# A four-layer network on one core: the deformable layer from windows to dense sampling matrices, the shift layer from one dense product to two block-diagonal ones

## The chip, the core and the metric

The kernel runs on one core of a Trainium2 chip (trn2). A core has a matrix engine (TensorE, "PE" in the profile, with its weight loads listed apart as "PEld"), a vector engine (VectorE, "DVE"), an activation engine (ScalarE, "ACT"), a general engine (GpSimd, "POOL") and a queue engine (SyncE, "SP") that only issues transfers here. Each engine works through its own list of instructions in order and waits on semaphores for the others. Transfers are carried out by 16 DMA engines; SP and ACT both issue them.

The metric is device time in microseconds, the median of three runs. The span in the profile goes from the first to the last instruction.

## The reference

An image batch x of shape (8, 384, 32, 32), fp32, goes through four layers, each of the form x = x + layer(group_norm(x)):

- Layer 0 is a selective state-space layer (Mamba) over the 1024 positions of an image, with 768 inner channels and 16 states.
- Layer 1 is a deformable layer. The 384 channels are split into three groups of 128, with kernel sizes K = 3, 5 and 7.
- Layer 2 is a state-space layer again, with layer norm before and an MLP behind.
- Layer 3 is a learned shift: the channels form 48 positions of 8 channels each; every position has its own displacement.

Layers 1 and 3 are the ones touched. Cut to the core:

```python
# layer 1, one group: K*K taps, each with its own offset field
offsets = conv2d(x, ow, ob, pad)                      # 2*K*K maps
for k in range(K * K):                                # ky, kx: the tap's place
    py, px = gy + ky + offsets[2*k], gx + kx + offsets[2*k+1]
    acc += bilinear_sample(x, py, px) * w[k]          # zero outside the image
out = conv2d(acc, pw, pb, 0)                          # pointwise
# all three groups: out * sigmoid(fc2(relu(fc1(mean))) + fc2(relu(fc1(max))))

# layer 3: integer displacement, then a depthwise 5x5 Gaussian, normalised
disp[c, y, x] = x[c, y - dy, x - dx]                  # zero outside
kernel = exp(-(|(j, i) + sub|**2) / (2 * 0.5**2)); kernel /= kernel.sum()
out = depthwise_conv(disp, kernel)
```

Bilinear sampling at (py, px) is a sum over all pixels (y, x) of the image with the weights max(0, 1 - |py - y|) times max(0, 1 - |px - x|). So a tap can be written as a product of the image, as a 128 channels x 1024 pixels matrix, with a 1024 x 1024 sampling matrix, in 8 tiles of 128 pixels. The Gaussian of layer 3 is a product of a factor in y and a factor in x.

## The kernel before

`tile_net` calls the layers one after the other; the images x1, x2 and x3 between them lie in DRAM. Instructions are written in program order against tiles from pools, and a framework places them on the engines' lists and inserts the waits. A tile of a pool with `bufs=n` comes free for its n-th successor when its last reader is done. The order of the lists is therefore fixed when the kernel is built.

**Layers 0 and 2** (`ssm_layer`, lines 139 to 292) loop over the 8 images; within an image over two groups of three blocks of 128 channels, and within those over the 16 states. Each step has an exponential on ACT (L231), a product on POOL (L233), a scan and a product on DVE (L234, L235) and an accumulation on TensorE (L237).

**Layer 1** is there twice. `deform_fast` is the one that runs. For every image and group it has preparation steps (`prep_steps`: group norm, the offset convolution L606, the positions L621, their store to DRAM L626, transposed copies of the image L657) and main steps (`main_steps`). It assumes that offsets are small (RAD: 2, 3 and 4 pixels). Up to four taps share the 128 partitions, 32 pixels each: a cell of 4 rows by 8 columns. Such a cell only reaches the output pixels in a window around it, so the sampling matrix is built and multiplied for the window alone: L717 and L722 make the row factor, L703 and L709 the column factor, L753 their product for the window (90 to 900 elements per partition), L736 the image times the tap's weight, and L767 the product into the accumulator. The preparation of the next block is placed between the main steps of the present one by costs and due times written in the code (PACE, FIRST, the costs of the steps). The largest offset of each block goes to `far`; after the loop it becomes a flag, which `tile_net` reads back. Only where it is set does `deform_layer` run, in a branch.

`deform_layer` and `deform_block` (lines 341 to 475) make no assumption on the offsets. A block convolves its group out of a padded copy, adds the grid, stores the positions `pos` to DRAM (`posd`), and transposes the image into 8 tiles `xt` of 128 pixels. Then, for each tap, it loads the two rows of positions broadcast to 128 partitions (`pyx`, 1 MB) and the tap's weights (`wk`), multiplies the image by the weights on POOL (`xk`), and builds the whole sampling matrix in three steps of 2, 3 and 3 tiles (STEPS): the first step takes its Relu on ACT, the others use two DVE instructions. Two products of 512 columns follow for every tile. The tiles `sm` have four buffers, `pyx`, `xk`, `wk` and `hx` two. In the profiled execution none of this ran.

**Layer 3** (`shift_layer`, lines 830 to 938) normalises and transposes all images into `xt` (lines 881 to 896). Per position the partitions hold 64 rows (8 channels x 8 images); the shift and Gaussian are one 1024 x 1024 matrix, built in 8 tiles from the factors in y and x (L929) and multiplied (L932, 16 products per position). The result is added to x (L936) and stored by 8 transfers of 32 KB (L938).

Of the kernel before, what the change touches and what calls it, by code (L numbers as in the profile page):

```python
# [8 lines left out]
F32 = mybir.dt.float32  # L9
AF = mybir.ActivationFunctionType  # L10
# [5 lines left out]
P = 128  # L16
# [15 lines left out]
CPP = 8  # L32
NT = L // P
# [3 lines left out]

RAD = {3: 2, 5: 3, 7: 4}  # L40
CONV = {3: (4, 32, L // 4), 5: (2, 64, HL), 7: (1, P, L)}
NCONV = {3: 1, 5: 4, 7: 14}
PACE = 1.6
FIRST = 9.8
NX = 4
NB = 5
HXN, HYN, SMN = 2080, 1792, 896

def box(y, x, h=2, w=2):
    return [(y + i, x + j) for i in range(h) for j in range(w)]


QUADS = {
    3: [box(-1, -1), [(-1, 1), (0, 1), (1, 0), (1, 1)], [(1, -1)]],
    5: [box(y, x) for y in (-2, 0) for x in (-2, 0)] + [box(2, -2, 1, 4), box(-2, 2, 4, 1), [(2, 2)]],
    7: [box(-3, -3), box(-3, -1), box(-1, -3, 1, 4), box(-3, 2), box(-1, 2), box(-3, 1, 4, 1)]
    + [box(0, -3), box(2, -3), box(0, -1, 4, 1), box(2, 0), box(2, 2), box(1, 0, 1, 4), [(0, 0)]],
}  # L60
# [9 lines left out]

def taps_of(K):
    return [(y + K // 2) * K + x + K // 2 for q in QUADS[K] for y, x in q]

# [5 lines left out]
class Net:  # L79
    def __init__(self, ctx: ExitStack, tc: tile.TileContext, ins, out, nb):  # L80
# [4 lines left out]
        self.mm = ctx.enter_context(tc.tile_pool(name="mm", bufs=2, space=PSUM))  # L85
        self.dram = ctx.enter_context(tc.tile_pool(name="dram", bufs=2, space=DRAM))
# [15 lines left out]
    def group_norm(self, x, xn):  # L102
# [26 lines left out]
        rstd = small.tile([P, G], F32, name="gn_rstd")  # L129
        nb = small.tile([P, G], F32, name="gn_nb")  # L130
# [3 lines left out]
        nc.vector.scalar_tensor_tensor(nb, grp[:, :, 0], -1.0, rstd, ALU.mult, ALU.mult)  # L134
        for g in range(G):
            nc.vector.tensor_scalar(
                xn[:, g, :], x[:, g, :], rstd[:, g : g + 1], nb[:, g : g + 1], ALU.mult, ALU.add
            )


    def ssm_layer(self, li, src, dst):
        tc, nc, ins = self.tc, self.nc, self.ins
        mlp = li == 2
        with ExitStack() as ctx:
# [3 lines left out]
            self.acc = ctx.enter_context(tc.tile_pool(name=f"acc{li}", bufs=3, space=PSUM))  # L148
# [191 lines left out]
    def deform_layer(self, src, dst):  # L340
        tc, nc, ins = self.tc, self.nc, self.ins
        with ExitStack() as ctx:
# [3 lines left out]
            self.acc = ctx.enter_context(tc.tile_pool(name="acc1", bufs=3, space=PSUM))  # L346
# [130 lines left out]
    def deform_fast(self, src, dst):  # L477
        tc, nc, ins = self.tc, self.nc, self.ins
        with ExitStack() as ctx:
            wp = ctx.enter_context(tc.tile_pool(name="w1f", bufs=1))  # L480
            self.q1 = ctx.enter_context(tc.tile_pool(name="q1", bufs=1))
            self.q2 = ctx.enter_context(tc.tile_pool(name="q2", bufs=2))
            self.win_acc = ctx.enter_context(tc.tile_pool(name="win_acc", bufs=1, space=PSUM))
            self.f = {}
            for g, K in enumerate(KS):
                K2, (n, st, cols) = K * K, CONV[K]
                rows = 2 * K2
                ow = wp.tile([P, K2, rows if n == 1 else st], F32, name=f"fow{K}")
                ob = wp.tile([P, 1], F32, name=f"fob{K}")
                obk = wp.tile([P, 1], F32, name=f"fobk{K}")  # L490
                grid = wp.tile([P, cols], F32, name=f"fgrid{K}")
                for t in (ob, obk, grid) + ((ow,) if n > 1 else ()):
                    nc.gpsimd.memset(t, 0.0)
                nc.sync.dma_start(out=ow[:, :, :rows], in_=ins[f"ow{K}"])
                for i in range(n):
                    r = slice(i * st, i * st + rows)
                    nc.sync.dma_start(out=ob[r], in_=ins[f"ob{K}"])
                    nc.sync.dma_start(out=obk[r], in_=ins["c_cols"][:rows, Q_K + g : Q_K + g + 1])
                    nc.sync.dma_start(out=grid[r], in_=ins["c_grid"][:rows, i * cols : (i + 1) * cols])
                nc.vector.tensor_tensor(obk, obk, ob, ALU.add)  # L500
                nq = K2 // 4
                wk = wp.tile([P, nq + 1, P], F32, name=f"fwk{K}")
                for t in range(4):
                    nc.sync.dma_start(
                        out=wk[H * t : H * (t + 1), :nq, :],
                        in_=ins[f"dw{K}"][t : 4 * nq : 4, :].partition_broadcast(H),
                    )
                nc.sync.dma_start(out=wk[:, nq, :], in_=ins[f"dw{K}"][4 * nq, :].partition_broadcast(P))

                nc.vector.tensor_scalar(wk, wk, -1.0, None, ALU.mult)  # L510
                self.f[K] = (ow, ob, obk, grid, wk)
            pwt = wp.tile([P, G, P], F32, name="pwt")
            nc.sync.dma_start(out=pwt, in_=ins["pw"].rearrange("g c o -> c g o"))
            pwb = wp.tile([P, G], F32, name="pwb")
            nc.sync.dma_start(out=pwb, in_=ins["pwb"])
            f1 = wp.tile([P, G, RK], F32, name="f1")
            nc.sync.dma_start(out=f1, in_=ins["fc1"].rearrange("(k p) o -> p k o", p=P))
            f2 = wp.tile([RK, C], F32, name="f2")
            nc.sync.dma_start(out=f2, in_=ins["fc2"])
            self.cell = wp.tile([P, 12], F32, name="cell")  # L520
            nc.sync.dma_start(out=self.cell, in_=ins["c_cell"])
            self.zero = wp.tile([P, HL], mybir.dt.bfloat16, name="zero")
            nc.gpsimd.memset(self.zero, 0.0)
            self.far = wp.tile([P, 4 * self.nb], F32, name="far")
            nc.gpsimd.memset(self.far, -1.0)


            mains, preps, at, now = [], [], [], 0.0
            state = {}
            for b in range(self.nb):  # L530
                for g in range(G):
                    s = {} if g else {"b": b}
                    state[g] = s
                    s["prev"] = state[0]
                    m = self.main_steps(b, g, s, (pwt, pwb, f1, f2), src, dst)
                    mains.append((now, m))
                    preps.append(self.prep_steps(b, g, s, src))
                    now += sum(c for c, _ in m)
            end = now
            for i in reversed(range(len(preps))):  # L540
                end = min(end, mains[i][0])
                first = mains[i - 1][0] + FIRST if i else 0.0
                for j, (cost, fn) in enumerate(reversed(preps[i])):
                    end -= PACE * cost

                    at.append((max(end, first) if j < 3 else end, i, fn))
            at.reverse()
            for i, (now, m) in enumerate(mains):
                for cost, fn in m:
                    while at and (at[0][0] <= now or at[0][1] <= i):  # L550
                        at.pop(0)[2]()
                    fn()
                    now += cost
            bad = self.small.tile([P, 1], F32, name="bad")
            nc.vector.reduce_max(bad, self.far, axis=AX.X)
            nc.vector.tensor_scalar(bad, bad, 0.0, None, ALU.is_gt)
            ones = self.small.tile([P, 1], F32, name="ones")
            nc.gpsimd.memset(ones, 1.0)
            ps = self.psum("ps_bad", rows=1, n=1)
            nc.tensor.matmul(ps, ones, bad, start=True, stop=True)  # L560
            flag = self.const.tile([1, 1], mybir.dt.int32, name="flag")
            nc.vector.tensor_copy(flag, ps)
            return flag

    @staticmethod
    def sub(ap, off, dims):
        return bass.AP(tensor=ap.tensor, offset=ap.offset + off, ap=[list(ap.ap[0])] + [list(d) for d in dims])


    def prep_steps(self, b, g, s, src):  # L570
        nc, K = self.nc, KS[g]
        K2, pad = K * K, K // 2
        n, st, cols = CONV[K]
        ow, ob, obk, grid, _ = self.f[K]

        def load():
            xn = self.q1.tile([P, G, L], F32, name="fxn")
            nc.sync.dma_start(out=xn, in_=src(b))
            self.group_norm(xn, xn)
            s["xn"] = xn  # L580

        def xg():
            return s["prev"]["xn"][:, g, :]


        taps = [(0, 0)] + [
            (y, x) for y in range(-pad, pad + 1) for x in range(-pad, pad + 1) if (y, x) != (0, 0)
        ]
        nh = 2 if n == 1 else 1
        m = HL if n == 1 else cols  # L590
        rows = m // W
        width = 2 * K2 if n == 1 else st
        used = width * n
# [439 lines left out]
```

## Time and profile before

| | |
|---|---|
| median of 3 runs | 16312.42 us (16312.03 to 16312.46) |
| profiled execution | 16312.03 us, span 16310.3 us |
| granted TensorE clock, mean | 0.803 of full |
| busy share of the span | PE 66%, DVE 74%, ACT 29%, POOL 30% |
| instructions | 92702 |

In a group row, "out<-in" names the tiles written and read, then come the shape of the output and input, the count, total busy time in us and the mean in ns of one instruction, and after the last bar the idle time of that engine just before them and what ended it. "fp32" products appear as two records each: L237 has 1536 x 2 products and 6144 records. A matmul's duration overlaps that of the next one, so the rate is read from the busy sum, which counts overlap once. Idle time of an engine that isn't the bottleneck costs nothing.

### The profile page before, as it was taken

How to read it: one execution, taken by the hardware profiler on the slowest of the kernel's cores; microseconds unless marked ns; L12 is line 12 of the kernel's file. 1: busy time of each engine (PE TensorE's matmuls, PEld its weight loads, DVE VectorE, ACT ScalarE, POOL GpSimd, SP SyncE). 2: the span in 40 equal slices, each digit the busy share in tenths (PEclk: the TensorE clock that was granted, in tenths of full speed). 3: DMA queues.
4: the chain of work that ended last, by engine and by line, in shares of the span. 5: the costliest groups of instructions: out<-in, count | busy, mean ns of one | idle time of the engine just before them, and what ended most of it. 6: DMA issues, size and time to landing. Idle time of an engine off the chain costs nothing. (4 is left out here: it accounts for less than half of the span.)

```text
span 16310.3 us, 92702 instructions
## 1 busy us (share of the span) xinstructions
PE 10784.7 (66%) x33010; PEld 5823.2 (36%) x33010; DVE 12014.2 (74%) x10304; ACT 4758.4 (29%) x6104; POOL 4889.3 (30%) x1652
## 2 busy tenths in 40 slices
PE   5545465454565698888885474747474747474699
PEld 2212122121221366666663141414141414141442
DVE  7787877878778678778887848484848484848577
ACT  2222222222222255555553222222222222222210
POOL 4454533535434200000002515151515152524200
PEclk7777777777776799999997787878787878786889
DMA  1111111111111222233332101010101010101111
GB/s 65 52 59 52 54 55 49 57 52 58 54 43 57 71 76 75 73 79 78 78 77 76 57 32 57 30 59 29 57 32 57 29 57 32 57 26 57 42 46 35
DMA packets 231328, 888.16 MB, mean 54 GB/s; under 512 B 33266, under 2 KB 41106, under 8 KB 207176
## 3 DMA queue, kind: packets, MB, share of 16 engines
q1 hardware_dynamic: 221000, 844.41, 16.6%
q10 hardware_dynamic: 9856, 37.75, 0.6%
q8 instruction: 261, 4.28, 0.1%
q14 instruction: 211, 1.73, 0.0%
HBM read 824.19 MB, written 57.87 MB: 54 GB/s over the span
## 5 line engine op out<-in xcount | busy, mean ns | idle before, releaser
L237 PE MATMUL y<-hs,ident 128*128 128x512 f32 x6144 | 4016.6, 818 | 4683.9 <-DVE hs L235 4683.9
L234 DVE TENSOR_TENSOR_SCAN hs<-da,hs 128x1024 f32<-128x1024 f32 x1536 | 5456.3, 3575 | 1112.2 <-POOL hs L233 1112.2
L233 POOL TENSOR_TENSOR hs<-du,bc 128x1024 f32<-128x1024 f32 x1536 | 4874.5, 3198 | 4615.4 <-PE y L237 3281.3
L237 PEld LDWEIGHTS y<-hs,ident 128*128 128x128 f32 x6144 | 1572.2, 267 | 7121.3 <-DVE hs L235 4890.8
L231 ACT ACTIVATE da<-dt,na 128x1024 f32<-128x1024 f32 x1536 | 1763.8, 1148 | 6492.8 <-DVE hs L234 6403.3
L235 DVE TENSOR_TENSOR hs<-hs,bc 128x1024 f32<-128x1024 f32 x1536 | 1951.7, 1295 | 16.5
L767 PE MATMUL wacc<-fsm,fxk 128*128 128x221 f32 (+34 forms) x10624 | 1680.6, 316 | 226.5 <-DVE fsm L753 220.8
L193 POOL MEMSET xp<- 128x2 f32 x96 | 10.0, 106 | 5701.7 <-ACTq L956 3169.4
L767 PEld LDWEIGHTS wacc<-fsm,fxk 128*128 128x128 f32 x10624 | 1580.4, 196 | 353.5 <-DVE fsm L753 260.9
L753 DVE TENSOR_TENSOR fsm<-fhy,fhx 128x170 f32<-128x170 f32 (+42 forms) x3216 | 1169.4, 426 | 261.0 <-PE wacc L767 255.7
L289 DVE SCALAR_TENSOR_TENSOR x<-ps_m,vec,x 128x256 f32<-128x256 f32 x96 | 46.4, 483 | 1191.4 <-PE ps_m L285 1191.4
L717 ACT ACTIVATE fhy<-fpyx,cell 128x416 f32<-128x416 f32 (+9 forms) x1280 | 655.3, 576 | 728.2 <-DVE fsm L753 728.2
L606 PE MATMUL ps_off<-fxn,fow 128*32 128x248 f32 (+19 forms) x2944 | 832.0, 522 | 2.1 <-issue 1.9
L736 DVE TENSOR_TENSOR fxk<-fxt,fwk 128x1024 f32<-128x1024 f32 x640 | 759.5, 1216 | 37.3 <-PE wacc L767 24.4
L932 PE MATMUL sacc<-sm,xt 128*64 128x512 f32 x1536 | 669.2, 597 | 32.6 <-DVE xr L936 31.7
L247 PE MATMUL ps_z<-xn,win 128*128 128x512 f32 x1152 | 582.1, 660 | 118.9 <-DVE dt L304 118.9
L197 PE MATMUL ps_in<-xn,win 128*128 128x512 f32 x1152 | 535.0, 625 | 50.9 <-DVE xn L331 34.6
L929 DVE TENSOR_TENSOR sm<-kr 128x1024 f32<-128x1024 f32 x384 | 463.6, 1221 | 135.6 <-PE sacc L932 135.5
L277 PE MATMUL ps_h<-xn,w 128*128 128x256 f32 x2304 | 504.6, 379 | 4.9 <-ACT hid L281 4.9
L285 PE MATMUL ps_m<-hid,w 128*128 128x256 f32 x2304 | 502.5, 379 | 0.0
L262 PE MATMUL ps_o<-u,wout 128*128 128x512 f32 x1152 | 497.0, 592 | 0.0
L606 PEld LDWEIGHTS ps_off<-fxn,fow 128*98 128x98 f32 (+2 forms) x2944 | 354.4, 147 | 377.6 <-issue 355.6
(163 smaller groups left out, 8299.5 us busy)
## 6 DMA issues: line engine op xcount, KB each, us to landing
bc<-bcd SPq DMA_DIRECT2D x512, 1024.0 KB
fpyx<-fposd SPq DMA_DIRECT2D x640, 256.0 KB
x<-x ACTq DMA_DIRECT2D x16, 1536.0 KB
fpyx<-fposd SPq DMA_DIRECT2D x24, 1024.0 KB
x<-x SPq DMA_DIRECT2D x16, 1536.0 KB
x<-in_x SPq DMA_DIRECT2D x8, 1536.0 KB
fxn<-x SPq DMA_DIRECT2D x8, 1536.0 KB
fxr<-x SPq DMA_DIRECT2D x24, 512.0 KB
```

Of the source, the lines that this page charges most:

```text
L231: nc.scalar.activation(da, dt[:, j, :], AF.Exp, scale=na[:, d0 + j, n : n + 1])
L233: nc.gpsimd.tensor_tensor(hs, du[:, j, :], bc[:, 0, :], ALU.mult)
L234: nc.vector.tensor_tensor_scan(hs, da, hs, 0.0, ALU.mult, ALU.add)
L235: nc.vector.tensor_tensor(hs, hs, bc[:, 1, :], ALU.mult)
L237: nc.tensor.matmul(ys[j][:, s], self.ident, hs[:, s], start=(n == 0), stop=(n == NS - 1))
L247: nc.tensor.matmul(ps, win[:, k, DI + d * P : DI + (d + 1) * P], xn[:, k, s], start=(k == 0), stop=(k == G - 1),)
L606: nc.tensor.matmul(o[:, ya - r0 : yb - r0, xa:xb], ow[:, (dy + pad) * K + dx + pad, :], x3[:, ya + dy : yb + dy, xa + dx : xb + dx], start ...
L717: nc.scalar.activation(hy[:, at : at + (yb - ya) * W], pyx[:, 0, ya * W : yb * W], AF.Abs, bias=bias)
L736: nc.vector.tensor_tensor(t, s[q], wk[:, j : j + 1, :].to_broadcast([P, 2 * NX, P]), ALU.mult)
L753: nc.vector.tensor_tensor(self.sub(sm, at, [(r * w, n), (w, r), (1, w)]), self.sub(hy, hy_at[by] + xa, [(r * W, n), (W, r), (1, w)]), self ...
L767: nc.tensor.matmul(a[:, ya - 4 * o : yb - 4 * o, xa:xb], k, self.sub(sm, sm_at[by], [(w, yb - ya), (1, w)]), start=False, stop=False,)
L932: nc.tensor.matmul(acc[:R, s], xt[:, t, p * R : (p + 1) * R], smf[:, s], start=(t == 0), stop=(t == NT - 1),)
```

## The change

The diff has two parts. In layer 1, `deform_fast`, `prep_steps`, `main_steps`, `excite`, their tables and the branch are taken out, and `deform_layer` is called for every run; its own code stays as it was, except that the PSUM pool `acc` is now made once for the network instead of once per layer (3 buffers as before). The taps of the weights are in their natural order again. In layer 3, the partitions hold four channels of one image at a time, 32 rows each (`(i y)`), and the free dimension 8 images x 2 channel quartets x 32 columns. The factor in y is a 128 x 128 block-diagonal matrix with four equal blocks of 32 x 32, and so is the factor in x. The first product contracts the rows and leaves the result transposed, with columns on the partitions; the second contracts the columns and turns it back. Group norm's scale and shift are gathered in a table `tab` and applied to the tile as it is loaded. `group_norm` is split, so that the statistics (`gn_stats`) can be taken alone. Layer 2 stores its result by image instead of by channel.

```diff
-    far = net.deform_fast(by_sample(x[1]), by_sample(x[2]))
-    with tc.If(net.nc.values_load(far[0:1, 0:1]) > 0):
-        net.deform_layer(by_sample(x[1]), by_sample(x[2]))
-    net.ssm_layer(2, by_sample(x[2]), by_channel(x3))
-    net.shift_layer(by_channel(x3), x3.rearrange("c b l -> (c b) l"), out)
+    net.deform_layer(by_sample(x[1]), by_sample(x[2]))
+    net.ssm_layer(2, by_sample(x[2]), by_sample(x[3]))
+    net.shift_layer(by_sample(x[3]), x[3], out)
...
-            xt = wp.tile([P, NT, C * nb], F32, name="xt")
...
-                self.group_norm(x, x)
+                self.gn_stats(x, rn[:, 0, b, :], rn[:, 1, b, :])
...
+            for t in range(2):
                 for g in range(G):
+                    nc.vector.tensor_tensor(
+                        sel, hi, rn[:, t, :, g].unsqueeze(2).to_broadcast([P, nb, nq]), ALU.mult
+                    )
+                    nc.tensor.matmul(
+                        ps, cst[:, T_LO : T_LO + P], sel.rearrange("p b q -> p (b q)"), start=True, stop=True
+                    )
+                    nc.scalar.copy(tab[:, t, g].rearrange("p b q -> p (b q)"), ps)
...
+                bd = p2.tile([P, M2, IG, W], F32, name="bd", tag="bd")
+                for i in range(IG):
+                    nc.scalar.activation(bd[:, :, i, :], kr, AF.Copy, scale=grp[:, i : i + 1])
                 for n in range(PC):
                     p = p0 + n
-                    nc.sync.dma_start(out=xr, in_=src[p * R : (p + 1) * R, :])
-                    for t in range(NT):
-                        nc.vector.tensor_tensor(sm, my, mx, ALU.mult)
-                        for h, s in halves():
-                            nc.tensor.matmul(
-                                acc[:R, s], xt[:, t, p * R : (p + 1) * R], smf[:, s],
-                                start=(t == 0), stop=(t == NT - 1),
-                            )
-                    nc.vector.tensor_tensor(xr, xr, acc[:R, :], ALU.add)
-                    for c in range(CPP):
-                        nc.sync.dma_start(out=dst[:, p * CPP + c, :], in_=xr[c * nb : (c + 1) * nb, :])
+                    xr = p2.tile([P, nb, NJ, W], F32, name="xr", tag="xr", bufs=3)
+                    for j in range(NJ):
+                        c = p * CPP + j * IG
+                        nc.sync.dma_start(
+                            out=xr[:, :, j, :],
+                            in_=src[:, c : c + IG, :].rearrange("b i (y x) -> (i y) b x", x=W),
+                        )
+                    for op, t in ((ALU.mult, 0), (ALU.add, 1)):
+                        nc.vector.tensor_tensor(
+                            xa, xr if t == 0 else xa,
+                            tab[:, t, g, :, q : q + NJ].unsqueeze(3).to_broadcast([P, nb, NJ, W]), op,
+                        )
+                    for k in range(0, HL, P):
+                        nc.tensor.matmul(ps[:, k : k + P], xaf[:, k : k + P], my, start=True, stop=True)
+                    nc.scalar.copy(yt, ps)
+                    for k in range(0, HL, P):
+                        nc.tensor.matmul(ps2[:, k : k + P], yt[:, k : k + P], mx, start=True, stop=True)
+                    nc.vector.tensor_tensor(xrf, xrf, ps2, ALU.add)
+                    for j in range(NJ):
+                        c = p * CPP + j * IG
+                        nc.scalar.dma_start(
+                            out=dst[:, c : c + IG, :].rearrange("b i (y x) -> (i y) b x", x=W),
+                            in_=xr[:, :, j, :],
+                        )
```

`deform_block`, which every image and group now goes through, has this loop over the taps (as it stood before, unchanged):

```python
for k in range(K2):
    pyx = p2.tile([P, 2, L], F32, name="pyx", tag="pyx")
    nc.sync.dma_start(out=pyx, in_=posd[2 * k : 2 * k + 2, :].partition_broadcast(P))
    ...
    nc.gpsimd.tensor_tensor(xk, xt, wk.unsqueeze(1).to_broadcast([P, NT, P]), ALU.mult)
    nc.scalar.activation(hx, pyx[:, 1, :], AF.Abs, bias=self.col(Q_XN))
    nc.scalar.activation(hx, hx, AF.Relu, bias=self.col(Q_ONE), scale=-1.0)
    for t0, t1, on_act in STEPS:                       # tiles 0-1, 2-4, 5-7
        for i in range(n):
            nc.scalar.activation(sm[:, i, :], pyx[:, 0, :], AF.Abs, bias=self.col(Q_YN + t0 + i))
        if on_act:
            nc.scalar.activation(sm, sm, AF.Relu, bias=self.col(Q_ONE), scale=-1.0)
            nc.vector.tensor_tensor(sm, sm, hxb, ALU.mult)
        else:
            nc.vector.tensor_scalar(sm, sm, 1.0, 0.0, ALU.subtract, ALU.min)
            nc.vector.scalar_tensor_tensor(sm, sm, -1.0, hxb, ALU.mult, ALU.mult)
        for i in range(n):
            for h, s in halves():
                nc.tensor.matmul(acc[:, s], xk[:, t0 + i, :], sm[:, i, s], ...)
```

## The prediction

> **What bounds the kernel now.** I read the 40 slices first, then cut the span at the four layers with the table of windows, then took unit costs from the groups by line. The four rows are layer 0 (state space), layer 1 (deformable), layer 2 (state space with MLP) and layer 3 (shift). Columns are start:end, length, busy time of PE, PEld, DVE, ACT and POOL with their instruction counts, granted TensorE clock, DMA share and GB/s.
>
> ```profile
> 0.00:5533.00 5533.00, 3077.45 (x5472) 1238.35 (x5472) 4367.55 (x2305) 1358.13 (x1338) 2438.41 (x826) 0.74 0.15 54
> 5533.00:8713.00 3180.00, 2764.24 (x15250) 2138.10 (x15250) 2482.55 (x4788) 1685.57 (x2825) 3.89 (x13) 0.94 0.30 78
> 8713.00:15437.00 6724.00, 4171.74 (x10271) 2147.31 (x10272) 4515.28 (x2511) 1616.83 (x1839) 2446.96 (x814) 0.78 0.13 45
> 15437.00:16310.30 873.30, 771.25 (x2018) 299.46 (x2016) 648.83 (x701) 97.83 (x102) 0.00 (x0) 0.91 0.17 46
> ```
>
> Layer 1 takes 3180 us with PE and DVE both near full, and POOL free; layer 3 takes 873 us and is TensorE's. The change touches only these two. The order of instructions of the changed kernel is the old one line for line in both state-space layers, so their 5533 + 6724 us stay.
>
> The unit costs, from the groups by line with shapes kept apart (count | busy us, mean ns | idle before):
>
> ```profile
> L262 PE MATMUL ps_o<-u,wout 128*128 128x512 f32 x1152 | 497.0, 592 | 0.0
> L929 DVE TENSOR_TENSOR sm<-kr 128x1024 f32<-128x1024 f32 x384 | 463.6, 1221 | 135.6 <-PE sacc L932 135.5
> L722 DVE TENSOR_SCALAR fhy<-fhy 128x1344 f32<-128x1344 f32 x80 | 68.1, 851 | 3.7 <-ACT fhy L717 3.7
> L722 DVE TENSOR_SCALAR fhy<-fhy 128x1600 f32<-128x1600 f32 x64 | 63.0, 984 | 16.6 <-ACT fhy L717 16.6
> L307 DVE SCALAR_TENSOR_TENSOR sp_e<-sp_w,sp_e 128x1024 f32<-128x1024 f32 x96 | 116.6, 1214 | 0.0
> L703 ACT ACTIVATE fhx<-fpyx,cols 128x1024 f32<-128x1024 f32 x24 | 27.6, 1148 | 4.6 <-DMA fpyx<-fposd 2.9 <-issue 1.7
> ```
>
> An fp32 product is two records: 576 products in L262, 497.0 us, so 0.86 us each back to back, loads hidden. Tensor-tensor runs at 1.04 ns an element; tensor-scalar at (984-851)/256 = 0.52, fixed part 0.15 us. And who holds up whom, from the tile view of hs (min/median/max ns):
>
> ```profile
> L233 POOL TENSOR_TENSOR hs<-du,bc x1536: 2330/2886/4439, 83.0 to 15255.5; 128x1024 f32<-128x1024 f32 x192
> L234 DVE TENSOR_TENSOR_SCAN hs<-da,hs x1536: 2257/4366/4483, 90.1 to 15264.1; 128x1024 f32<-128x1024 f32 x192
> ```
>
> The scan takes 2.26 us alone and 4.37 beside a POOL product: it stands still for 2.11 us, nearly the whole POOL instruction.
>
> **What the Trainium skill says.** "SBUF — State Buffer", section Who interferes with whom: GpSimd's one SBUF port pair is VectorE's second; a VectorE instruction with two SBUF inputs, or in a two-port mode, and a GpSimd one that reads SBUF exclude each other for a whole instruction. The 2.26/4.37 us above agree. "VectorE: DVE Perf Modes", section The perf-mode tier table: fp32 tensor-scalar has a 2x mode, tensor-tensor none; 0.52 against 1.04 ns agree. "TensorE: Matmul & The Clock Gate", section Part 1: The HAM clock gate: an idle TensorE drops to half clock and needs some 3.4 us of work to come back; the 0.74 of layer 0 and 0.94 of layer 1 fit. "DMA: Bandwidth & Descriptors", section Specifications: line rate needs runs of 512 B or more, below it a read-modify-write is done. Loads here do well with less (200-byte runs of the weights fow: 2125 packets in 2.2 us, nearly all engines busy, about 15 ns each on 16 engines); short stores do not occur.
>
> **Part A, layer 1: windows out, dense sampling in.** Removed: 3180 us with everything in it, also the planned interleaving of the next block's convolution with the present block's taps, and the flag that `tile_net` reads back at its end. Added: `deform_block` 24 times, with 83 taps per image, so 664 taps. One tap costs, engine by engine:
>
> PE: 16 products of 128x512 at 0.86 = 13.7 us.
>
> DVE: one tensor-tensor of 2048 elements, then twice a tensor-scalar and a scalar-tensor-tensor of 3072. Back to back, an instruction starts N x 1.04 ns + 0.07 us after the one before (two L736 of 1024 take 2.34 us). So 2.20 + 2 x (1.75 + 3.27) = 12.24 us; the 1.75 is the full 0.52 x 3072 + 0.15, since the next instruction reads its result.
>
> POOL: the product xk, 1024 elements like L233: 2.33 us alone. All five DVE instructions have two SBUF inputs or the 2x mode, so by the lock it adds 2.1 us to DVE: 14.35 us.
>
> ACT: ten activations of 1024, one of 2048. Four L717 of 416 take 1.97 us with 0.63 for one, so a start every 0.45 = 416 x 0.833 ns + 0.10. Thus 0.95 per 1024, 1.81 for 2048, one wait of 0.2: 11.5 us. Its 1 MB of positions per tap is 73 GB/s, less than layer 1 moves now.
>
> DVE and POOL together set the beat, PE close behind at 13.7; I take 14.5 with waits. 664 x 14.5 = 9628 us.
>
> Between blocks nothing overlaps: on PE the order is convolution, transposes, all taps, pointwise product, next convolution. The convolutions are 166 products per image: 166 x 0.86 x 8 = 1140 us, in which DVE, ACT and POOL have nothing to do. Around each: last 6 products and backlog 6.4, copy of the accumulator 1.3 (L936: 1.2), pointwise 1.7; then pos 1.0, its store 2.3 (8478.84 to 8481.13 in the timeline), the 1 MB broadcast back 5.0 (8481.13 to 8486.14), five activations and the Relu of 2048 until the first DVE product 6.8: 24.5 us x 24 = 588. At an image's end the excitation chain and the group norm of the next image stand in line on DVE and PE ahead of the convolution: og 0.4 more, two reductions 2.4, two small products with Relu 2.5, norm matrices 2.9 + 4.0 (as at 15587), three products into x 3.8, normalise 2.3, padding copies 0.7, small steps 2: 21 x 7 = 147. Weights and first image 40 (as now), last excitation to layer 2's first statistics 28. Sum 9628 + 1140 + 588 + 147 + 68 = 11571 us, against 3180: **+8391 us**.
>
> **Part B, layer 3.** Removed: 384 dense tiles, 768 products of PE (660 us), 48 x 1.2 us additions, 384 stores of 32 KB; transposes and normalising of x in preparation. Layer 2's store changes from channel-major to sample-major, same 4 KB rows: nothing, hidden under the next image's work.
>
> Added: preparation, statistics only. PE has 2.9 + 4.0 us of tiny products per image with 1.1 us of DVE between, 8 us x 8 = 64; before it 20 for loads (as now), 26 for the table, the first chain and the first position: 110. Then 48 positions, each: DVE three passes of 512 at about 0.68 (L781: 684 ns) plus a quarter of five passes of 256 = 2.6 us; PE eight products of 128x128 at 0.27 (eight ps_t records, 1.06 us) = 2.1; ACT 0.59 copy, 0.7 for kernels and block diagonals, two DMA issues at 0.4 = 2.1. ACT stands in order, copy, then the stores that wait for DVE's addition, which waits for the second product: copy 0.6, PE 1.2, DVE 0.7, issues 0.8, waits: about 4 us. DMA: each load and store has 1024 runs of 128 B, 64 per engine, four per position. At 15 ns all: 3.8 us; if short stores cost four times that, my estimate of the penalty that the skill names, 2 x 64 x 60 + 1.9 = 9.6. I take 6 us; ends 4 and 15. 48 x 6 = 288, end 5. Sum 403 against 873: **-470 us**.
>
> Total: 16312.0 for the profiled execution (span 16310.3 and 1.7 outside; the median 16312.42 is the same within 0.4) + 8391 - 470 = **24233 us**.
>
> **Rivals.**
> (1) As above: DVE with POOL sets the tap, 14.5 us. 24233. Own range 23.7 to 24.8 ms. Chance 0.5.
> (2) The xk product hides: it runs while DVE waits anyway, and TensorE sets the tap at 13.8 us. For it: PE's 13.7 is above DVE's 12.24. Against: the scan of 4.37 us. 664 x 0.7 less: 23770. Chance 0.2.
> (3) Three engines in a chain through four sm buffers, all 80 to 95% busy, don't overlap fully; the half clock after each gap of some 15 us puts PE behind. At 16 us a tap: +1000, 25230. Chance 0.23.
> (4) Layer 3's 128-byte stores run at 15 us a position, ACT stuck behind them: +430, 24660. It may join any of these; alone 0.06.
> (5) Not slower: only layer 3's saving counts, 15840. It needs layer 1 dense in 3180 + 470 us; after 1940 us of convolutions and gaps that leaves 1710 / 664 = 2.6 us a tap, where the 16 products alone are 13.7. It would take products five times faster than any row shows, or a dense layer that isn't run; but its call stands outside any branch now. Chance 0.01.
>
> **How the numbers follow.** The time is that of (1). The range joins (2), (1), (3) and part of (4): 13.3 to 16.2 us a tap are -800 and +1130 around 24233, and the high end takes 340 of layer 3's +430 with it: 23400 to 25700. Faster than 0.2% only in (5): 0.01; within 0.2% (about what a measurement of this kernel can tell from no change) 0.0; slower 0.99.
>
> **What would show it.** Layer 1's window should be some 11.6 ms long, with DVE near 85% busy inside the taps; scalar-tensor-tensor at 3.35 us or 5.4 where POOL's product fell on it; xk at 2.3 to 5 us; PE clock near full in the taps; 24 gaps of DVE, each of 0.86 us x 2 x (9, 25 or 49) + 24. If DVE's 3072-element tensor-scalar takes 3.3 us instead of 1.75, the two-port mode isn't granted and a tap is 17.5. In layer 3, the interval between two stores of xr gives the 6 us directly. I am wrong if tap intervals are far from 14.5, or if convolutions overlap taps after all.

## The result: 24292 us against 16312 us

The changed kernel takes 24291.7 us (median of 4 runs, 24290.4 to 24292.8) against 16312.4 us for the kernel before beside it, a ratio of 1.489 with a 95% interval of 1.487 to 1.492. The profiled execution's span is 24288.4 us; predicted were 24231.3 us for the span and 24233 us for the time. The forecast is 57 us short of the profiled span, 0.2%, but that small number is the sum of several larger misses of both signs, which the experiments below take apart.

The table of windows of the changed kernel, cut at the four layers, answers to the one shown of before (columns as there: length, busy time of PE, PEld, DVE, ACT, POOL, granted TensorE clock, DMA share, GB/s).

```profile
0.00:5533.00 5533.00, 3048.98 (x5472) 1236.57 (x5472) 4357.77 (x2304) 1358.73 (x1338) 2448.22 (x822) 0.74 0.15 54
5533.00:17202.20 11669.20, 10648.29 (x24576) 4493.56 (x24576) 9742.24 (x3711) 8483.64 (x7395) 2474.66 (x690) 0.97 0.18 67
17202.20:23926.30 6724.10, 4176.91 (x10272) 2149.41 (x10272) 4518.14 (x2512) 1616.19 (x1839) 2445.45 (x814) 0.78 0.13 45
23926.30:24288.40 362.10, 235.99 (x1068) 211.23 (x1068) 160.21 (x352) 71.90 (x146) 0.00 (x0) 0.61 0.57 110
```

Layers 0 and 2 kept their times to about 1 us: the last VectorE instruction of layer 0 ends at 5533.3 us before and at 5533.7 after, and VectorE's part of layer 2 takes 6731.7 and 6731.0 us. (The borders in the tables are placed by hand, so equal lengths there show no more than this.) Layer 1 went from 3180 to 11669 us (+8489, predicted +8391); layer 3 from 873 to 362 us (-511, predicted -470).

What a tap of layer 1 looks like is told by the timeline of the changed kernel. L435 is the tensor-tensor product of the first step, L437 and L438 are the tensor-scalar and the scalar-tensor-tensor of the other two steps, L423 is GpSimd's product and L441 TensorE's. The rows show one period of VectorE, GpSimd and TensorE with other rows left out (start, duration, engine, line, operation; in brackets the idle time before and who ended it):

```profile
8998.58 3.36 DVE L438 SCALAR_TENSOR_TENSOR sm<-sm,hx 128x3072 f32<-128x3072 f32 x1
9000.34 3.82 POOL L423 TENSOR_TENSOR xk<-xt,wk 128x1024 f32<-128x1024 f32 x1 [10.68 <-PE dacc L441]
9001.85 3.93 DVE L437 TENSOR_SCALAR sm<-sm 128x3072 f32<-128x3072 f32 x1
9005.81 3.36 DVE L438 SCALAR_TENSOR_TENSOR sm<-sm,hx 128x3072 f32<-128x3072 f32 x1
9009.09 2.28 DVE L435 TENSOR_TENSOR sm<-sm,hx 128x2048 f32<-128x2048 f32 x1
...
9009.32 13.97 PE L441 MATMUL dacc<-sm,xk 128*128 128x512 f32 x32 [0.53 <-DVE sm L438]
9011.29 1.75 DVE L437 TENSOR_SCALAR sm<-sm 128x3072 f32<-128x3072 f32 x1
...
9023.59 2.28 DVE L435 TENSOR_TENSOR sm<-sm,hx 128x2048 f32<-128x2048 f32 x1
```

From one L435 to the next it is 9023.59 - 9009.09 = 14.50 us, the interval between taps (the beat) that was predicted. GpSimd's product becomes ready at 9000.34, when TensorE gives a buffer of xk free. It can't start then: a scalar-tensor-tensor with two SBUF inputs is running. That one ends at 9001.9, GpSimd runs, and the tensor-scalar behind it takes 3.93 instead of 1.75 us. TensorE idles 0.53 us per tap for VectorE.

The groups by line of the changed kernel (count | busy us, mean ns | idle before, releaser), from its page:

```profile
L441 PE MATMUL dacc<-sm,xk 128*128 128x512 f32 x21248 | 9320.7, 597 | 848.1 <-DVE sm L435 535.0
L423 POOL TENSOR_TENSOR xk<-xt,wk 128x1024 f32<-128x1024 f32 x664 | 2443.3, 3681 | 7333.4 <-PE dacc L441 6772.2
L438 DVE SCALAR_TENSOR_TENSOR sm<-sm,hx 128x3072 f32<-128x3072 f32 x1328 | 4459.8, 3358 | 45.7
L437 DVE TENSOR_SCALAR sm<-sm 128x3072 f32<-128x3072 f32 x1328 | 3665.2, 2760 | 0.0
L435 DVE TENSOR_TENSOR sm<-sm,hx 128x2048 f32<-128x2048 f32 x664 | 1516.1, 2283 | 483.1 <-ACT sm L434 483.1
L399 PE MATMUL ps_off<-xpf,ow 128*98 128x512 f32 (+2 forms) x2656 | 1180.3, 605 | 55.4 <-DVE xpf L391 49.8
```

L437's mean of 2760 ns is a mixture: 616 of the 1328 took some 2.18 us longer, (1328 x 1.754 + 616 x 2.18) / 1328 = 2.76. The 616 are all taps but two in each of the 24 blocks, because the first two products of a block are made before VectorE starts. In the whole trace it is always the second of a tap's two tensor-scalars that is stalled, and GpSimd's product always became ready during the scalar-tensor-tensor before it; L438 itself never took longer than 3.36 us. L435's 483.1 us of idle time before it are 20.1 us in the mean of the 24 block starts (18.7 to 21.3).

### The profile page after: what moved, and what is told of

It is laid out like the page before. It is cut to its first block, busy times and chain, and to the rows that moved or that the text cites. A ratio compares the mean times of both kernels' runs of the same rounds, so it can differ in the third digit from the quotient of the medians.

```text
span 24288.4 us, 119417 instructions
## 1 busy us (share of the span) xinstructions
PE 18110.2 (75%) x41388; PEld 8090.8 (33%) x41388; DVE 18778.4 (77%) x8878; ACT 11530.5 (47%) x10718; POOL 7368.3 (30%) x2326
## 5 line engine op out<-in xcount | busy, mean ns | idle before, releaser
L441 PE MATMUL dacc<-sm,xk 128*128 128x512 f32 x21248 | 9320.7, 597 | 848.1 <-DVE sm L435 535.0
L441 PEld LDWEIGHTS dacc<-sm,xk 128*128 128x128 f32 x21248 | 4004.3, 191 | 6150.4 <-issue 5980.0
L432 ACT ACTIVATE sm<-pyx,cols 128x1024 f32<-128x1024 f32 x5312 | 5718.5, 1135 | 89.5 <-PE dacc L441 39.0
L423 POOL TENSOR_TENSOR xk<-xt,wk 128x1024 f32<-128x1024 f32 x664 | 2443.3, 3681 | 7333.4 <-PE dacc L441 6772.2
L438 DVE SCALAR_TENSOR_TENSOR sm<-sm,hx 128x3072 f32<-128x3072 f32 x1328 | 4459.8, 3358 | 45.7
L437 DVE TENSOR_SCALAR sm<-sm 128x3072 f32<-128x3072 f32 x1328 | 3665.2, 2760 | 0.0
L435 DVE TENSOR_TENSOR sm<-sm,hx 128x2048 f32<-128x2048 f32 x664 | 1516.1, 2283 | 483.1 <-ACT sm L434 483.1
L434 ACT ACTIVATE sm<-sm,cols 128x2048 f32<-128x2048 f32 x664 | 1329.2, 2002 | 20.0
L399 PE MATMUL ps_off<-xpf,ow 128*98 128x512 f32 (+2 forms) x2656 | 1180.3, 605 | 55.4 <-DVE xpf L391 49.8
L426 ACT ACTIVATE hx<-hx,cols 128x1024 f32<-128x1024 f32 x664 | 762.4, 1148 | 19.3
```

The lines of the kernel that those rows point to most:

```text
L423: nc.gpsimd.tensor_tensor(xk, xt, wk.unsqueeze(1).to_broadcast([P, NT, P]), ALU.mult)
L432: nc.scalar.activation(sm[:, i, :], pyx[:, 0, :], AF.Abs, bias=self.col(Q_YN + t0 + i))
L434: nc.scalar.activation(sm, sm, AF.Relu, bias=self.col(Q_ONE), scale=-1.0)
L435: nc.vector.tensor_tensor(sm, sm, hxb, ALU.mult)
L437: nc.vector.tensor_scalar(sm, sm, 1.0, 0.0, ALU.subtract, ALU.min)
L438: nc.vector.scalar_tensor_tensor(sm, sm, -1.0, hxb, ALU.mult, ALU.mult)
```

## Experiments on layer 1: what sets the beat, and what the gaps are

Theory 1 is the prediction's own: VectorE and GpSimd exclude each other, and their sum sets 14.5 us. The rival, theory 2, is its case (2): TensorE, 13.8 us of products per tap, sets the beat anyway.

**GpSimd's product left out** (TensorE takes xt unweighted):

```
-            nc.gpsimd.tensor_tensor(xk, xt, wk..., ALU.mult)
...
-                            acc[:, s], xk[:, t0 + i, :], sm[:, i, s],
+                            acc[:, s], xt[:, t0 + i, :], sm[:, i, s],
```

> The changed kernel with GpSimd's product xk left out: TensorE takes the transposed image xt as it is, so the taps' weights are missing from the result; nothing else differs. Theory 1 (GpSimd's product shuts VectorE out once per tap, and the two together set the beat of 14.50 us): a tap falls to what TensorE needs, 13.8 to 14.0 us; VectorE's second tensor-scalar goes from 3.93 back to 1.75 us. Over 664 taps, less what the first and last tap of each of the 24 blocks save already, that is 350 to 470 us off 24292: 23820 to 23940 us. Theory 2 (TensorE sets the beat already, VectorE's wait for GpSimd lies in time that it would idle anyway): nothing, within 50 us of 24292.

Measured: 23883.8 us, 408 less. **The same product on VectorE**, in full:

```
-            nc.gpsimd.tensor_tensor(xk, xt, wk..., ALU.mult)
+            nc.vector.tensor_tensor(xk, xt, wk..., ALU.mult)     # xk bufs=3, xpf bufs=1
```

> The changed kernel with the product xk computed on VectorE instead of GpSimd, with three buffers for xk and one for the padded image; the result is the full one. Theory 1: VectorE has 12.24 + 1.13 = 13.4 us of work per tap and nobody that shuts it out, so TensorE's 13.8 to 14.0 us set the beat, as without the product: 23820 to 24000 us. Theory 2 (the 14.50 us have another cause than the shut-out): VectorE gets 1.1 us longer per tap, and its wait stays: up to 750 us slower, 24300 to 25040 us.

Measured: 23756.4 us, 535 less, though VectorE has 1.1 us more to do per tap; that is 64 us below the range of theory 1, so the shorter tap alone does not explain it. **Half of the products left out**, on all taps but the first of a block:

```
                     for h, s in halves():
+                        if h == 1 and k > 0:
+                            continue
...
```

> The changed kernel with the second half of the sampling products left out on all taps but the first of each block: TensorE has 8 instead of 16 products per tap, 7 us instead of 13.8; the second half of the positions is incomplete. Theory 1: VectorE's 12.24 us and the 2.17 us for which GpSimd shuts it out still make 14.4 us per tap; at most 60 us from the taps and up to 100 us from the shorter backlog at the end of the 24 blocks go: 24130 to 24260 us. Theory 2 (TensorE sets the beat): a tap falls to VectorE's 12.3 to 13 us, 1000 to 1400 us off: 22900 to 23300 us.

Measured: 24203.3 us, 88 less. Fifty microseconds from the middle of a 49-tap block show the three cases side by side. First the changed kernel's table of windows, then that without the product, then that with half of the products (columns as above):

```profile
8990.00:9040.00 50.00, 47.88 (x110) 20.41 (x110) 49.76 (x18) 43.03 (x38) 11.45 (x3) 1.00 0.20 68
```

```profile
8980.00:9030.00 50.00, 50.00 (x117) 22.07 (x117) 45.41 (x19) 46.54 (x41) 0.00 (x0) 1.00 0.21 84
```

```profile
8990.00:9040.00 50.00, 30.54 (x55) 11.70 (x54) 49.76 (x18) 45.09 (x40) 16.23 (x4) 0.86 0.20 68
```

In the changed kernel VectorE is busy 49.76 of 50 us (a blocked instruction counts as busy). With half of TensorE's work gone VectorE still is, at the same 49.76, and a tap still takes 14.49 us (9026.37 to 9040.86 between two L435): TensorE doesn't set the beat. With GpSimd's product gone TensorE is busy 50.00 of 50, and a tap takes 13.73 us (9011.76 to 9025.49): then TensorE does set it. Theory 2 falls; the mutual exclusion costs 0.77 us per tap, the distance from 14.50 to the next bound.

One thing did not fit: leaving the product out gained 127 us less than moving it. The weight loads wk no longer had a reader in that run, nothing held them back, and SyncE's queue was full of them, first between the loads of the positions and then ahead of their store. From its timeline of SyncE (two taps, and the block start behind them; in the changed kernel the store goes out some 30 us earlier):

```profile
5663.14 14.73 SPq L421 DMA_DIRECT2D wk<-in_dw  x10
5677.91 0.43 SPq L419 DMA_DIRECT2D pyx<-posd  x1
...
5712.90 114.86 SPq L421 DMA_DIRECT2D wk<-in_dw  x79
5827.81 0.36 SPq L405 DMA_DIRECT2D posd<-pos  x1
```

**Product and weight loads both left out** (the edit above, and the load of wk with it):

> The changed kernel without GpSimd's product and also without the loads of the tap weights, which nothing read any more in the run without the product alone; the weights are missing from the result. Theory 1 (in that run the loads without a reader filled SyncE's queue ahead of the store of the positions and lengthened the gaps; the tap itself was TensorE's 13.73 us): the gaps shrink, 23700 to 23770 us. Theory 2 (the run without the product was slower than that with the product on VectorE for another reason in the taps): 23860 to 23900 us.

Measured: 23692.1 us, 600 less than the changed kernel, 192 less than without the product alone, and 8 us below the range of theory 1. So the queue had hidden part of the gain; the run of 23884 lay in its expected range partly by this accident. But theory 1 looked for it in the gaps between the blocks, and the larger part was elsewhere: in the run without the product alone, 38 taps of the first image took 16.9 us instead of 13.73, some 120 us in all, with ten weight loads between two loads of positions as in the lines above. In the run without the weight loads no tap takes over 13.8 us, and the remaining 70 us are in the gaps. That the gain exceeded the range also suggests that the weight loads cost something in the changed kernel. There, at each of the 24 block starts, two of them stand between the store of the positions and the first load of them back. This is the timeline of one (SyncE's queue and the first instructions that wait for it):

```profile
5795.59 0.30 SPq L405 DMA_DIRECT2D posd<-pos  x1
...
5799.40 2.62 SPq L421 DMA_DIRECT2D wk<-in_dw  x2
5802.13 0.85 SPq L419 DMA_DIRECT2D pyx<-posd  x2
5809.62 1.15 ACT L425 ACTIVATE hx<-pyx,cols 128x1024 f32<-128x1024 f32 x1 [12.72 <-DMA pyx<-posd]
...
5816.85 2.29 DVE L435 TENSOR_TENSOR sm<-sm,hx 128x2048 f32<-128x2048 f32 x1 [21.28 <-ACT sm L434]
```

The two loads are for taps 2 and 3; their buffers come free when GpSimd has made the products of taps 0 and 1. **Four buffers for wk:**

```
-            wk = p2.tile([P, P], F32, name="wk", tag="wk")
+            wk = p2.tile([P, P], F32, name="wk", tag="wk", bufs=4)
```

> The changed kernel with four buffers for the tap weights wk instead of two. In the gap before each block's taps two weight loads, for taps 2 and 3, stand in SyncE's queue between the store of the positions and the first load of them back, and wait until GpSimd has made the products of taps 0 and 1. Theory 1 (this wait is part of the 6 us by which a gap is longer than predicted): with four buffers they don't wait, the first load goes out some 3 us earlier, 24 gaps: 50 to 80 us less than 24292, 24212 to 24242 us. Theory 2 (the gap is set by the store's and the broadcast's own time): no change, within 10 us.

Measured: 24294.7 us, no change. But the edit had not done what it should. The timeline of that run has the same wait in the same place:

```profile
5793.40 2.62 SPq L421 DMA_DIRECT2D wk<-in_dw  x2
5796.13 31.66 SPq L419 DMA_DIRECT2D pyx<-posd  x4
```

With four buffers the loads are put two taps further ahead, and the two in that place, for taps 4 and 5, wait for the same two products. **The loads in another queue** takes them out of the way:

```
-            nc.sync.dma_start(out=wk, in_=ins[f"dw{K}"][k, :].partition_broadcast(P))
+            nc.gpsimd.dma_start(out=wk, in_=ins[f"dw{K}"][k, :].partition_broadcast(P))
```

> The changed kernel with the loads of the tap weights wk issued from GpSimd's queue instead of SyncE's. With four buffers the two loads ahead of the first pyx were those of taps 4 and 5 and waited for the same two products, so the wait was still there; now SyncE has only the store of the positions and the loads of them back. Theory 1 (the wait is part of the 6 us by which a gap is longer than predicted): the first load goes out 2.6 to 4 us earlier in 24 gaps, 50 to 90 us less than 24292: 24202 to 24242 us. Theory 2 (store and broadcast set the gap by themselves): within 10 us of 24292.

Measured: 24154.2 us, 137.5 less, more than expected. Its timeline at the same block start, and its group of L435:

```profile
5788.59 0.29 SPq L405 DMA_DIRECT2D posd<-pos  x1
...
5791.25 0.80 SPq L419 DMA_DIRECT2D pyx<-posd  x2
5796.10 1.15 ACT L425 ACTIVATE hx<-pyx,cols 128x1024 f32<-128x1024 f32 x1 [6.21 <-DMA pyx<-posd]
```

```profile
L435 DVE TENSOR_TENSOR sm<-sm,hx 128x2048 f32<-128x2048 f32 x664 | 1516.3, 2284 | 335.9 <-ACT sm L434 335.9
```

Store to first load is 2.66 us instead of 6.54, and the load lands after 4.85 instead of 7.49 us: I had thought of the wait in the queue only, not that the first positions also land sooner once the 64 KB broadcasts are not ahead of them. In the mean of the 24 block starts the two steps are 2.53 instead of 6.53 us and 4.65 instead of 6.78 us, together the 6.1 us by which the idle time per block start fell, from 20.1 to 335.9 / 24 = 14.0 us. That the broadcasts are the cause of the second step too is not shown by a run that changes it alone, but the trace fits: in the 3 us after the first load of positions is issued, the DMA engines of the changed kernel are only 0.28 busy, and 135 of their 158 packets are smaller than 2 KB; with the weights in GpSimd's queue they are 0.68 busy, and no packet is.

With the weight loads out of the way worth 137 us, the exclusion alone is worth 600 - 137 = 463 us, against 350 to 470 expected; 616 taps times 0.77 us are 474. The run with the product on VectorE had both in part, which fits its result below the range: its first load of positions leaves 3.05 us after the store (9009.14 to 9012.19).

**One tap of the offset convolution instead of 9, 25 or 49:**

```
-            for k in range(K2):
+            for k in (K2 // 2,):
```

> The changed kernel with one tap of the offset convolution instead of 9, 25 or 49 (the other taps are left out, so the offsets are others; the sampling has the same work wherever it looks). Theory 1 (nothing runs beside the convolutions, each stands fully on the path): 160 products per image fewer at 0.86 to 0.88 us, 8 images: 1050 to 1130 us off, 23160 to 23240 us. Rival (part of the convolution hides behind the last products of the block before or the preparation of the next): less than 600 us off, above 23690 us.

Measured: 23187.8 us, 1104 less. 1280 products fewer in all, 0.86 us each. L399's busy time fell by 1120 us, from 1180.3 to 60.4, so the convolutions stand on the path all but in full.

## Experiments on layer 3: additivity, and what sets a position

**The new shift layer alone**, the deformable layer left as before (the split group norm, `shift_layer` and the constants taken over; layer 2 stores by sample):

> The kernel before with the new shift layer alone (layer 2's store sample by sample, statistics, table and block-diagonal products as in the changed kernel); the deformable layer stays with its windows. The two parts add up: 873.3 - 362.1 = 511 us off 16312, 15801 us, within 15 us. Rival (the two parts act on each other, through the state of the clock or of the queues at the layers' borders): off by over 15 us from that; the sum of the prediction would put it at 15842.

Measured: 15803.8 us against 16309.4 beside it, ratio 0.969 (0.967 to 0.971). The parts add up: this half of the change is a gain of 3%, and the whole loss is the other half's.

The prediction gave a position 6 us. From the tile view of xr, the additions L570 of the 48 positions start from 24044.2 to 24283.5, so 239.3 / 47 = 5.09 us. The groups by line, shapes apart, say who waits:

```profile
L554 DVE TENSOR_TENSOR xa<-xr,tab 128x512 f32<-128x512 f32 x48 | 33.2, 691 | 97.6 <-DMA xr<-x 97.0 <-PE ps_y L563 0.6
```

VectorE waits 2 us per position for the load of xr. Two readings: the transfers are slow (runs of 128 B), or they start late (three buffers of xr, each held from its load until its store has read it). **Six buffers, long runs, and both:**

```
-  xr = p2.tile([P, nb, NJ, W], F32, name="xr", tag="xr", bufs=3)
+  xr = p2.tile([P, nb, NJ, W], F32, name="xr", tag="xr", bufs=6)
```

```
-  in_=src[:, c : c + IG, :].rearrange("b i (y x) -> (i y) b x", x=W)
+  in_=src.rearrange("b c l -> (b c l)")[p * P * HL : (p + 1) * P * HL]
+      .rearrange("(q f) -> q f", f=HL)[:, j * HL // 2 : (j + 1) * HL // 2]   # out= and the stores alike
```

> As the new shift layer alone, with six buffers instead of three for xr. Theory A (the loop of three buffers sets a position's 4.9 us: load, sum, store and the wait until the store has read it take 14.7 us together): a position falls to what the DMA engines or ScalarE's line need, 3.4 to 4.2 us, 34 to 72 us less than the new shift layer alone. Theory B (the 4096 runs of 128 B per position keep the DMA engines full): no change, within 10 us.

> As the new shift layer alone, with three buffers, but each position loads and stores one stretch of 256 KB in runs of 1024 B per partition instead of its channels in runs of 128 B; the same bytes and the same number of issues, other elements, so the result is another. Theory A (loop of three buffers): the transfers' part of the loop gets shorter, a position takes 3.2 to 4.5 us, 20 to 80 us less. Theory B (the runs of 128 B are the bound): the bound goes, and a position falls to ScalarE's line of about 4 us: 40 us less; in the trace the DMA share of the positions falls from 0.69 to 0.3 or below.

> As the new shift layer alone with six buffers for xr, and in addition the runs of 1024 B (other elements, so the result is another). Theory A (with six buffers the 128 B runs became the bound, DMA engines 0.91 busy): a position falls from 3.7 us to the line on ScalarE and VectorE, 3.0 to 3.5 us, 10 to 33 us less than with six buffers alone: 15709 to 15732 us, DMA share 0.5 or less. Theory B (the line copy, product, addition, two issues on ScalarE sets the 3.7 us): within 5 us of 15742.

| new shift layer alone, and | time, us | a position, us | DMA share | TensorE clock |
|---|---|---|---|---|
| three buffers, runs of 128 B | 15803.8 | 5.11 | 0.70 | 0.62 to 0.66 |
| three buffers, runs of 1024 B | 15761.6 | 4.23 | 0.36 to 0.43 | 0.66 to 0.97 |
| six buffers, runs of 128 B | 15741.9 | 3.82 | 0.91 | 0.90 to 0.93 |
| six buffers, runs of 1024 B | 15725.2 | 3.49 | 0.48 | 1.00 |

A position is the distance of the first to the last addition over 47; the shares and clocks are from two windows of 50 us among the positions. For the three-buffer kernel, then the six-buffer kernel, both with runs of 128 B:

```profile
15600.00:15650.00 50.00, 35.04 (x158) 30.76 (x157) 23.52 (x41) 10.61 (x22) 0.00 (x0) 0.62 0.70 106
```

```profile
15600.00:15650.00 50.00, 30.59 (x213) 27.81 (x213) 32.71 (x56) 16.69 (x36) 0.00 (x0) 0.90 0.91 135
```

Three buffers are the bound in the kernel as it is: the same runs of 128 B go through faster as soon as there are six, which theory B excludes. Long runs with three buffers help too, 42 us, but a shorter loop would give that as well as a lifted bound, so that run alone could not tell the theories apart; its DMA share stayed above the 0.3 that theory B named. With six buffers the DMA engines are 0.91 busy, and long runs then take off another 17 us, as theory A said. With six buffers and runs of 128 B TensorE gains too: its idle stretches get shorter, the granted clock rises from 0.62 to 0.90, and the mean record of the first product falls from 409 to 296 ns. How much of the 62 us is this and how much the buffers by themselves, the runs don't separate.

The version with six buffers computes everything and is the fastest that does: 15741.9 us, 0.965 (0.963 to 0.967) of the kernel before.

## Why the prediction was right, by its steps

- **The tap, 14.5 us from DVE 12.24 and POOL's 2.1.** Right, in the mechanism and in the number: 14.50. A little luck is in the number: the 0.15 us added "with waits" stood for waits that are not there, and made up for two terms that were each 0.08 to 0.09 us too small (12.33 + 2.18 = 14.51). VectorE's sum without GpSimd is 12.33 where it can be seen (5816.85 to 5829.18, the first tap of a block). TensorE without other bounds takes 13.73 (13.7 predicted). The conflict always fell on the tensor-scalar, not on the scalar-tensor-tensor as my sign "3.35 or 5.4" had it; and VectorE is not near 85% busy in the taps but 49.76 of 50 us, since the blocked time counts as busy.
- **664 x 14.5.** Too much by 104 us: two products of each block are made in the gap, so 48 taps take 12.33: 616 x 14.50 + 48 x 12.33 = 9524 us instead of 9628.
- **24 gaps of 24.5 us.** Too short. The part from the store to the first product was 14.1 us and was 20.1: +144 us. The step that failed is "its store 2.3, the 1 MB broadcast back 5.0": nothing was counted between them, and two weight loads stand in the queue there. With them in another queue the runs give 14.0 us, so the other terms were right in their sum. The backlog, copy and pointwise product took 10.2 (5740.81 to 5751.03) instead of 9.4 us: +19.
- **Convolutions, 1140 us, all exposed.** Exposed, yes. The records of L399 sum to 1180: +38. About half of it is the blocks with K = 3, which come after an idle stretch: their 144 products take 142.9 us, 0.99 us each, at a granted clock of 0.92 in the block at 7028.39. The other half is that the 1184 products of the larger blocks take 0.88 us each, not 0.86 (687.4 + 350.0 us), with the granted clock at 1.00 in the block at 5751.03.
- **Image ends, 21 us.** 19.7 in the first (7008.65 to 7028.39): -9, if the others are alike. All these make -104 + 144 + 19 + 38 - 9 = +88 of the +98 us by which layer 1 was longer.
- **ScalarE, 11.5 us.** Activations of 1024 follow each other at 1.04 us (5810.67 to 5811.71), not 0.95. That came from a misread row: the timeline merges instructions and shows the form of the first, so the "four L717 of 416" at 6201.76 have 416, 416, 320 and 192 elements, and the two of 416 start 0.54 us apart, not 0.45. It is about 12.5 us per tap (43.03 of 50 us busy). Off the path at 14.5.
- **Layer 3, 403 us.** The preparation with the first position took 118 us to its addition (23926.3 to 24044.2), 110 predicted: +8. The positions, 48 x 6 = 288 predicted, were 47 more at 5.09: 239, -49. The step "I take 6 us" was the middle between a line of 4 us on ScalarE and transfers of up to 9.6. Neither was it: the loop of three buffers was, a wait that the sum had no term for. The mis-sized term is the penalty on short stores: at the rates below, the transfers come to 3.4 us instead of 9.6.
- **Rivals.** (2) falls with the half-products run. (3), the loss in the chain through four sm buffers, is not there: without GpSimd's product TensorE runs without a pause. (4) is not there either. From 24050 to 24280 us ScalarE's queue, which has the stores, takes 34.1% of the 16 engines for 93557 packets, and SyncE's, which has the loads, 32.5% for 92671: 0.341 x 16 x 230 us / 93557 = 13.4 ns per packet of a store and 12.9 ns of a load, where 60 and 15 were counted (the prediction's own row, 2.2 us x 16 / 2125, gives 16.6 for the 15). (5): layer 3's saving alone is 15804, and layer 1 did cost 8489.

## What to carry to other kernels

Where GpSimd and VectorE exclude each other as here, add GpSimd's product to VectorE's sum, then compare with the next bound: what can be gained by moving it is only the distance to that bound, here 0.77 of the 2.18 us. Price a hand-over through DRAM in the order of its queue, with all that stands between the store and the load, and when an edit shows nothing, look whether the wait has gone before dropping the theory. A row that a timeline has merged carries the form of its first instruction only; take a unit cost from a group with one form. A wait for a load that is ended by a DMA can mean late starts as well as slow transfers; here DMA engines that were only 0.70 busy spoke for late starts, and the run with six buffers showed it.

## What was not expected of the hardware

- A GpSimd product that waits behind a VectorE instruction gets the shared ports, of which the Trainium skill says in "SBUF — State Buffer", Who interferes with whom, that one holds them for a whole instruction, before VectorE's next one, although that is ready: in the changed kernel all 616 products that fall into the taps let the running scalar-tensor-tensor end (3.36 us, 3358 ns in the mean) and stall the tensor-scalar behind it (3.93 us).
- Runs of 128 B cost stores hardly more than loads: 13.4 against 12.9 ns per packet; with six buffers a run takes, over both directions, 0.91 x 16 x 3.82 / 4096 = 13.6 ns, against 0.48 x 16 x 3.49 / 512 = 52 ns per run of 1024 B. An eighth of the bytes thus costs a quarter of the time.
- GpSimd's queue could issue the weight loads beside a VectorE that is 49.76 of 50 us busy (8900 to 8950): 1.37 us in the mean (0.53 to 1.45), and a tap stayed at 14.50 us (9005.49 to 9019.99).
